# Normalized tokens split over the partition halves, so that the projections run in 64-row tiles of TensorE

## Chip, cores and metric

One core of one Trainium2 chip runs the whole program in one launch. The metric is the device time of that launch in microseconds; the time before is the median of three runs.

## What is computed

A transformer block in fp32 on `x` (2 batches of 1024 tokens, 256 features) with a context of 154 tokens of 192 features. There are 16 heads of 64, so an attention is 1024 wide.

```python
h = layernorm(x, ln1_g, ln1_b)
x = attention(h, h, sa_wq, sa_wk, sa_wv, sa_wo, sa_bo) + x
h = layernorm(x, ln2_g, ln2_b)
x = attention(h, ctx, ca_wq, ca_wk, ca_wv, ca_wo, ca_bo) + x
h = layernorm(x, ln3_g, ln3_b)
p = h @ ff_w1 + ff_b1                      # 2 x 1024 wide
x = (p[..., :1024] * gelu(p[..., 1024:])) @ ff_w2 + ff_b2 + x
# attention: q, k, v by heads; softmax(q k^T / 8) v; then @ wo + bo
```

## The kernel before

**Units.** A unit is one batch and one pair of heads: 16 units, 8 a batch. Self attention takes them in order, and each unit has 8 slots `p` (two halves `h` of 4), so there are 128 slots. In a slot `self_first` (L534) writes two score blocks, each 128 query rows (4 groups of 32) by two heads by 512 keys: 8 matmuls in tiles of 64 rows and 32 columns of TensorE's array (L382), with the head choosing the row half and the bank. The two halves of the keys of one query group lie in different groups of 32 rows, so that maxima and sums are exchanged between partitions by four small DMAs on SP (`exchange`, L403) and joined a slot later (`join`, L407: GpSimd, and an exponential `ee` on ScalarE). VectorE takes the maxima (L542), ScalarE the exponentials (L393), GpSimd scales the weights (L493), VectorE transposes them in blocks of 32 (L507), and two slots behind, `self_values` (L511) multiplies them with the values in 64x64 tiles (`weigh`, L429).

**What fills TensorE between the scores.** In slots 2, 3, 6 and 7 of a unit `self_values` runs for the half before. In slots 0, 1, 4 and 5 (all of the first four slots of all) `run_work` (L452) takes pieces from the list `work`: the projections of the *next* unit, in the order q, q, k, k, v, v (`self_pieces`, L329), each with one PSUM bank of 512 columns (`mm_tile`, two of them in turn). Then, as far as the slot's budget of banks goes, it takes pieces of the output projection from `outs` (L355), and one step of `side`: parts of the next layer norm (`norm_beside`, L267). What a piece leaves in PSUM is copied by ScalarE at the start of the next slot (`stores`, `flush`).

**Projections.** `project_half` (L293) makes queries or keys of 512 tokens: two matmuls of 512 columns over 128 features each, weights stationary, in 128x128 tiles. `project_self_values` (L310) makes 4 token tiles of values: 2 matmuls of 128 columns each, tokens stationary. The values are then copied by two DMAs on SP to the other partition half (L324, L325). An fp32 matmul shows as two records with two weight loads in the profile.

**Layer norm.** `norm_pieces` (L180): statistics by tile of 128 tokens on VectorE, deviation on GpSimd, normalization on ScalarE (L218), four 128x128 transposes for two tiles on TensorE (`turn`, L223), then two stores of 128x256 with gain and shift per partition (L236, L240). The normalized, transposed tokens `hT` have 128 features on the partitions, two chunks of them, and 1024 tokens.

**Weights.** The slices of a unit (256 features by 128 columns, 128 KB for each of q, k, v) come by `load_pair` (L123) into a pool of two buffers, two units ahead, at the unit's first slot (`self_beside`, L554).

**Cross attention.** A unit has three slots with context scores in 64x128 tiles (`cross_first`, L647), 64x64 products with the values (`cross_values`, L721), and the pieces of the next unit: q, q, keys, and values every second unit (`cross_pieces`, L592; `cross_beside`, L756). The feed-forward part follows; its normalized tokens keep their layout.

## Time and profile before

| | us |
|---|---|
| median of three runs (1159.74 to 1162.74) | 1160.25 |
| the profiled execution, its own time | 1161.83 |
| its span | 1160.1 |
| first scores start | 18.4 |
| self attention, units 4 to 14 | 198.7 to 684.7 |
| last unit of self attention | 684.7 to 725.7 |
| cross-attention loop | 725.7 to 961.1 |
| feed-forward | 961.1 to 1160.1 |

TensorE's granted clock was full throughout. A row of a timeline has the start, the length, the engine (PE is a matmul, PEld a weight load), the line, the operation, what it writes and reads, the array tile (64*32 is 64 rows by 32 columns), the shape and the count; in brackets stand idle time before it and what ended it. Matmuls are pipelined and the length of a group contains a modelled tail, so the difference of two starts is what a group takes. A row of a stage table has the stretch, its length, and for each engine its busy time and number of instructions, then granted clock, DMA share and GB/s.

### The profile page before, as it was taken

What the parts mean: (1) busy time and instruction counts of PE and PEld (TensorE: products, weight loads), DVE (VectorE), ACT (ScalarE), POOL (GpSimd) and SP (SyncE); (2) the same over time, 40 slices, a digit from 0 to 9 for tenths busy, and PEclk for the clock granted to TensorE, in tenths of its full rate; (3) what the DMA queues carried; (4) which work ended last, traced back from release to release, by engine and by line L of the source; (5) the groups of instructions that cost most, each with busy time, mean ns of one, the idle gap of its engine ahead of it and who ended that gap; (6) DMA issues with size and microseconds to landing.
All of it is one profiled execution on the core that took longest, in us unless ns stands there. A gap on an engine that the chain in (4) does not pass through costs nothing.

```text
span 1160.1 us, 31720 instructions
## 1 busy us (share of the span) xinstructions
PE 1134.3 (98%) x11931; PEld 675.6 (58%) x11931; DVE 833.0 (72%) x1178; ACT 643.4 (55%) x2055; POOL 665.9 (57%) x1556
## 2 busy tenths in 40 slices
PE   8989999999999999999999999999999999999998
PEld 6334444545545545545445444565666667888887
DVE  4888999898889888888999889557656664232222
ACT  4656677666656665665666766547755572041111
POOL 1767777887877777777777777546654453020000
PEclk9999999999999999999999999999999999999999
DMA  2311011101101111011011010157544433000000
GB/s 76 92 52 34 12 25 35 21 17 31 24 21 22 25 25 21 17 34 21 17 34 21 18 29 5 33 138 195 126 107 103 104 84 71 10 10 10 19 10 18
DMA packets 87250, 51.21 MB, mean 44 GB/s; under 512 B 30830, under 2 KB 77882, under 8 KB 87098
## 3 DMA queue, kind: packets, MB, share of 16 engines
q1 hardware_dynamic: 83738, 46.44, 17.4%
q10 hardware_dynamic: 3360, 2.76, 0.8%
q8 instruction: 94, 1.54, 0.6%
q14 instruction: 58, 0.48, 0.1%
HBM read 19.52 MB, written 2.10 MB: 19 GB/s over the span
## 4 chain that ended last, share of the span: by engine, by line
PE 80%; ACT 7%; DVE 4%; POOL 3%; DMA 2%; issue 2%; SPq 1%; DVEq 0%; ACTq 0%; POOLq 0%
PE po L429 17%; PE s L382 15%; PE pa L824 10%; ACT p L393 5%; PE py_ca L360 5%; PE pf L847 5%; PE py_sa L360 5%; PE pq_ca L299 4%; PE poc L737 4%; PE pk_sa L299 4%; PE pq_sa L299 3%; PE pv_sa L315 3%; PE sc L658 3%; DVE st L542 2%; DMA st<-st 2%
## 5 line engine op out<-in xcount | busy, mean ns | idle before, releaser
L393 ACT ACTIVATE p<-s,st 128x512 f32<-128x512 f32 x512 | 345.2, 686 | 220.7 <-DVE st L542 214.1
L493 POOL TENSOR_SCALAR p<-p,rd,ee 128x512 f32<-128x512 f32 x512 | 385.6, 767 | 44.3 <-DVE rd L489 43.7
L542 DVE TENSOR_REDUCE st<-s 128x2 f32<-128x1024 f32 x256 | 301.3, 1218 | 45.8 <-PE s L382 38.5
L507 DVE STREAM_TRANSPOSE pT<-p 128x1024 f32<-128x1024 f32 x256 | 302.4, 1219 | 1.5 <-POOL p L493 1.5
L382 PE MATMUL s<-k_sa,q_sa 64*32 64x512 f32 x4096 | 253.9, 596 | 14.2 <-ACT p L393 13.1
L429 PE MATMUL po<-pT,v_sa 64*64 64x256 f32 x4096 | 235.8, 379 | 0.0
L429 PEld LDWEIGHTS po<-pT,v_sa 64*64 64x64 f32 x4096 | 150.4, 133 | 109.2 <-issue 38.6
L685 POOL TENSOR_SCALAR p<-p,rden 128x154 f32<-128x154 f32 x256 | 96.8, 399 | 108.8 <-DVE rden L682 108.3
L382 PEld LDWEIGHTS s<-k_sa,q_sa 64*32 64x32 f32 x4096 | 59.9, 105 | 145.1 <-ACT p L393 53.8
L674 ACT ACTIVATE p<-sc,neg 128x154 f32<-128x154 f32 x256 | 96.0, 395 | 83.6 <-DVE rden L682 79.4
L824 PE MATMUL pa<-hT_ln,wf 128*128 128x256 f32 x512 | 121.0, 379 | 0.0
L833 DVE SCALAR_TENSOR_TENSOR u<-pa,cols,gate 128x256 f32<-128x256 f32 x64 | 31.0, 484 | 124.2 <-ACT gate L830 124.2
L830 ACT ACTIVATE gate<-pa,cols 128x256 f32<-128x256 f32 x64 | 30.3, 474 | 151.4 <-PE pa L824 151.4
L824 PEld LDWEIGHTS pa<-hT_ln,wf 128*128 128x128 f32 x512 | 96.8, 190 | 13.7 <-DVE u L833 0.4
L393 ACT ACTIVATION_READ_ACCUMULATOR p<-s,st 128x1 f32 x512 | 103.7, 203 | 0.0
L663 DVE TENSOR_REDUCE neg<-sc 128x6 f32<-128x924 f32 (+1 forms) x48 | 48.5, 1011 | 48.6 <-PE sc L658 48.6
L417 POOL TENSOR_TENSOR zz<-ee,st 128x8 f32<-128x8 f32 x128 | 25.8, 202 | 80.3 <-ACT ee L415 80.3
L315 PEld LDWEIGHTS pv_sa<-sa_wv,hT_ln 128*128 128x128 f32 x512 | 59.1, 192 | 15.8 <-issue 14.1
L847 PE MATMUL pf<-wf,u 128*128 128x256 f32 x256 | 65.0, 379 | 0.2 <-DVE u L833 0.2
L315 PE MATMUL pv_sa<-sa_wv,hT_ln 128*128 128x128 f32 x512 | 62.2, 278 | 0.0
L299 PE MATMUL pq_ca<-hT_ln,ca_wq 128*128 128x512 f32 x128 | 60.0, 608 | 1.6 <-ACT v_ca L632 0.8
L299 PE MATMUL pk_sa<-hT_ln,sa_wk 128*128 128x512 f32 (+1 forms) x132 | 60.5, 596 | 0.6 <-ACT q_sa L308 0.6
(74 smaller groups left out, 1234.6 us busy)
## 6 DMA issues: line engine op xcount, KB each, us to landing
wf<-pT_ca SPq DMA_DIRECT2D x128, 128.0 KB, 2.4
st<-st SPq DMA_DIRECT2D x512, 1.0 KB, 1.7
v_sa<-v_sa SPq DMA_DIRECT2D x64, 128.0 KB, 2.5
wf<-in_L_xattn_ff_w_dram SPq DMA_DIRECT2D x12, 256.0 KB, 3.9
sa_wq<-in_L_xattn_sa_wq_dram SPq DMA_DIRECT2D x16, 128.0 KB, 3.5
sa_wk<-in_L_xattn_sa_wk_dram SPq DMA_DIRECT2D x16, 128.0 KB, 2.3
sa_wv<-in_L_xattn_sa_wv_dram SPq DMA_DIRECT2D x16, 128.0 KB, 2.9
ca_wq<-in_L_xattn_ca_wq_dram SPq DMA_DIRECT2D x16, 128.0 KB, 2.6
```

The costliest lines, as they stand in the source:

```text
L299: nc.tensor.matmul(pq[:, own], lhsT=wt[:, c, :], rhs=h[:, c, n * HB + own.start:n * HB + own.stop], start=(c == 0), stop=(c == NC - 1),)
L315: nc.tensor.matmul(pv[:, i * P:(i + 1) * P], lhsT=h[:, c, (n * GT + i) * P:(n * GT + i + 1) * P], rhs=wt[:, c, :], start=(c == 0), stop=(c ...
L360: nc.tensor.matmul(py[:, :D], lhsT=o[:, i, t * P:(t + 1) * P], rhs=wo[kind][:, half * HP + i, :], start=(i == 0), stop=(i == HP - 1),)
L382: nc.tensor.matmul(sc[a4 * KB:(a4 + 1) * KB, j, :], lhsT=q[r, c:c + KB], rhs=k[r, h * HB:(h + 1) * HB], start=True, stop=True, tile_positi ...
L393: nc.scalar.activation(pr[:, j, :], sc[:, j, :], AF.Exp, bias=st[:, 0, 0, i, j:j + 1], accum_out=st[:, 0, 1, i, j:j + 1],)
L429: nc.tensor.matmul(po[a2][j * DH:(j + 1) * DH, :QH // 2], lhsT=v[r, t, e, j * DH:(j + 1) * DH], rhs=pT[r, j * NK + n, :], start=(t == 0 an ...
L493: nc.gpsimd.tensor_scalar(pr[:, j, :], pr[:, j, :], rd[:, c:c + 1], ee[:, 0, c:c + 1], op0=ALU.mult, op1=ALU.mult,)
L507: nc.vector.transpose(halves[h][:, :, c:c + KB], groups.pop(0).rearrange("p j (n k) -> p (j n) k", k=KB))
L542: nc.vector.tensor_reduce(st[:, 0, 0, i, :], sc[i], AX.X, ALU.max, negate=True)
L685: nc.gpsimd.tensor_scalar(pr_[:, j, i, :T], pr_[:, j, i, :T], rden[:, j, i:i + 1], 1.0, op0=ALU.mult, op1=ALU.mult,)
L824: nc.tensor.matmul(pa[:, half, :TF * P], lhsT=w1[:, c, half * DF + f * P:half * DF + (f + 1) * P], rhs=h[:, c, t0 * P:(t0 + TF) * P], star ...
L847: nc.tensor.matmul(sums[blk][i][:, :D], lhsT=sums[blk, "u"][:, f, i * P:(i + 1) * P], rhs=w2[:, f, :], start=(f == 0), stop=(f == NF - 1),)
```

## The change

The tokens of a batch are split in two halves of 512, and `hT` of the self and context norms becomes four chunks of 64 features: partitions 0 to 63 hold them for the first half of the tokens, partitions 64 to 127 for the second. The transposes stay four for two tiles, since tile i and tile i + 4 are turned together (`tile_order`), and the stores become four of 128x128. Gains and shifts of these two norms are loaded twice, once for each partition half, and so are the slices of the weights, by two DMAs each; their pool goes from two buffers to one.

Queries and keys are projected by `project_both`: for each chunk of 64 features, four groups of 32 output columns and two token halves, a matmul of 512 columns in a 64x32 tile; the two token halves write two banks. In the first unit it uses 64x128 tiles and 256 tokens of each half at a time. Context queries use it in 64x128 tiles, save those of the first context unit, which are made beside self attention, in 64x32. Values are made in 64x128 tiles: tokens of a half stationary, two banks. A piece now has a cost in banks (`costing`), 2 for these pieces, and `run_work` counts it, so that a slot takes one of them. For units 1 to 4 the values stay in two pieces of half the size, with four copy DMAs each; later units have one piece and two larger copies.

The weight loads leave the unit's first slot: `load_ahead` issues q in slot 2, k in slot 3, v in slot 7 of a unit, two units ahead. Context keys and values are loaded one unit ahead, context queries two units ahead in the second of the three slots. The start loads `cols` by four DMAs. In the last self-attention unit two output pieces join `outs` that were listed in the second cross slot before.

```diff
-    wpool = ctx.enter_context(tc.tile_pool(name="w", bufs=2))
+    wpool = ctx.enter_context(tc.tile_pool(name="w", bufs=1))
...
+        t = wpool.tile([P, NH, n], F32, tag=name[3:], name=f"{name}_{c0}")
+        for r0 in range(0, P, HR):
+            nc.sync.dma_start(out=t[r0:r0 + HR], in_=own.rearrange("(c p) f -> p c f", p=HR))
+        return t
...
         def store():
-                for c in range(NC):
-                    own = st["hT"][:, c, t * P:(t + 2) * P]
+                k = NC * 2 * P // nh
+                for c in range(nh):
+                    own = st["hT"][:, c, t // 2 * k:(t // 2 + 1) * k]
...
+    def project_both(dst, pq, wt, h, m, t0=0, n=S // 2, mul=None):
+        for c in range(NH):
+            for f in range(0, P, m):
+                for r in range(2):
+                    own = slice(r * HR, (r + 1) * HR)
+                    nc.tensor.matmul(
+                        pq[r][f:f + m, t0:t0 + n], lhsT=wt[own, c, f:f + m],
+                        rhs=h[own, c, t0:t0 + n], start=(c == 0), stop=(c == NH - 1),
+                        tile_position=(r * HR, f),
+                    )
...
+    def project_self_values(v, pv, wt, h, i0, n):
+        for i in range(i0, i0 + n):
+            for c in range(NH):
+                for r in range(2):
+                    own = slice(r * HR, (r + 1) * HR)
+                    nc.tensor.matmul(
+                        pv[r][:, i * P:(i + 1) * P], lhsT=h[own, c, i * P:(i + 1) * P],
+                        rhs=wt[own, c, :], start=(c == 0), stop=(c == NH - 1),
+                        tile_position=(r * HR, 0),
+                    )
...
+            for own in [slice(0, NT)] if n == GT else tiles:
+                nc.sync.dma_start(out=v[:QG, own, 1, :], in_=v[QG:, own, 0, :])
+                nc.sync.dma_start(out=v[QG:, own, 1, :], in_=v[:QG, own, 0, :])
...
-        for _ in range(min(n, len(work))):
+        while n > 0 and work:
+            n -= work[0].banks
             run(work.pop(0))
-            n -= 1
...
+    def load_ahead(p):
+        ui, n = divmod(p, 2 * SH)
+        for what in "qkv":
+            at = {"q": 2, "k": 3, "v": 2 * SH - 1}[what] + 3 * (ui == 0 and what != "v")
+            if n != at:
+                continue
+            if ui + 2 < NU:
+                load_weights("sa", units[ui + 2][1], what)
+            elif ui + 2 == NU or what == "q":
+                load_weights("ca", units[ui + 2 - NU][1], what)
...
-                full = (hg % 2 == 0 or outs) and p < SA - 2 * SH
-                run_work(2 if full else 1, 1, sum_tile)
+                run_work(2 if p < SA - SH else 1, 1, sum_tile)
...
         if ui + 1 < NU:
+            for what in "kv":
+                load_weights("ca", units[ui + 1][1], what)
             pieces = cross_pieces(*units[ui + 1])
-            work.extend(pieces[:3])
-            held.extend(pieces[3:])
+            work.extend(pieces[:2])
+            held.extend(pieces[2:])
```

## Prediction

> **What bounds the kernel now.** I read the engine shares first, then the busy time by stage, then the order of TensorE's work in time. The engine shares:

> ```profile
> PE 1134.3 (98%) x11931; PEld 675.6 (58%) x11931; DVE 833.0 (72%) x1178; ACT 643.4 (55%) x2055; POOL 665.9 (57%) x1556
> ```

> 98% is an average. The stages (columns: stretch, its length, then busy time of PE, PEld, DVE, ACT, POOL) say where TensorE has room: units 0; 1 to 3; 4 to 14 of self attention; the cross-attention loop.

> ```profile
> 18.40:63.70 45.30, 42.98 (x510) 20.43 (x510) 33.36 (x34) 28.78 (x82) 24.03 (x54) 1.00 0.35 90
> 63.70:198.70 135.00, 127.04 (x1704) 60.07 (x1697) 121.08 (x142) 90.33 (x265) 101.06 (x230) 1.00 0.11 23
> 198.70:684.70 486.00, 485.82 (x6330) 251.78 (x6326) 432.91 (x481) 309.03 (x916) 364.66 (x815) 1.00 0.12 24
> ...
> 725.70:961.10 235.40, 230.26 (x1824) 146.74 (x1821) 146.80 (x326) 142.00 (x619) 124.02 (x346) 1.00 0.47 112
> ```

> From 198.7 on TensorE never rests; DVE has 53 us to spare. In units 1 to 3 PE is idle for 8 us and DVE for 14, so the two take turns. What one TensorE slot is made of, from its timeline (start, length, group):

> ```profile
> 268.59 1.95 PE L382 MATMUL s<-k_sa,q_sa 64*32 64x512 f32 x32
> 270.46 3.72 PE L360 MATMUL py_sa<-sa_wo,o_sa 128*128 128x256 f32 x16
> 274.11 1.95 PE L382 MATMUL s<-k_sa,q_sa 64*32 64x512 f32 x32
> ...
> 285.10 1.95 PE L382 MATMUL s<-k_sa,q_sa 64*32 64x512 f32 x32
> 286.98 3.70 PE L299 MATMUL pq_sa<-hT_ln,sa_wq 128*128 128x512 f32 x8
> 290.61 1.95 PE L382 MATMUL s<-k_sa,q_sa 64*32 64x512 f32 x32
> 292.48 3.70 PE L299 MATMUL pk_sa<-hT_ln,sa_wk 128*128 128x512 f32 x8
> ```

> Read differences of starts; the lengths hold a modelled tail. And where two pieces of one tile form follow each other (no change of form):

> ```profile
> 962.85 3.62 PE L360 MATMUL py_ca<-ca_wo,o_ca 128*128 128x256 f32 x16
> 966.30 1.89 PE L824 MATMUL pa<-hT_ln,wf 128*128 128x256 f32 x8
> ```

> The same 16 records of 256 columns take 3.45 us there (0.842 ns a column) and 3.65 between scores. A change of form in and out costs this piece 0.20. Two score calls are 4 passes of 512 columns, 1.72 us at that rate, and take 1.87: 0.15 more. A query piece is 3.45 at that rate and takes 3.63: 0.18 more. So the two changes of form in a query or key slot cost 0.15 + 0.18 = **0.33 us**.

> [...]

> **The change, part by part.**

> *Queries and keys in 64x32 tiles.* Per unit, 2 x 8 records of 512 columns become 2 x 64, eight at a time: 64/8 x 512 = 4096 columns, 3.45 us as before. Loads grow from 8 to 64 a piece, 32 columns each. The row of the score loads shows that they overlap (4096 of 105 ns in 59.9 us busy):

> ```profile
> L382 PEld LDWEIGHTS s<-k_sa,q_sa 64*32 64x32 f32 x4096 | 59.9, 105 | 145.1 <-ACT p L393 53.8 <-issue 52.9 <-ACT ee L415 29.8
> ```

> Issue: 64 matmuls and 64 loads in 3.45 us is the pace that a po piece already keeps (64 and 64 in 3.62[...]). What goes is both changes: 0.33. Queries and keys issued in units 4 to 14 are 22 pieces, plus unit 15's first context query: 23 x 0.33 = **-7.6 us**. Bounds: 0 (another cause for the 0.33) and 23 x 0.38, if the rate is a little better.
> Who is late next: DVE runs back to back from 81.92 to 86.94, 5.02 us a slot; the query slot falls from 5.50 to 5.17, still above.

> *Context queries in 64x128 tiles, the form of the context scores (sc).* 16 records of 512, two at a time: 3.45 again. They stand between two sc pieces:

> ```profile
> 847.06 1.06 PE L658 MATMUL sc<-k_ca,q_ca 64*128 64x154 f32 x12
> 848.05 3.70 PE L299 MATMUL pq_ca<-hT_ln,ca_wq 128*128 128x512 f32 x8
> 851.68 1.06 PE L658 MATMUL sc<-k_ca,q_ca 64*128 64x154 f32 x12
> ```

> 15 pieces x 0.33 = -5.0. Against it: a piece now needs both banks free before it starts. In the rows of waits pq_ca already waited 0.84 for ACT's v_ca copies and 0.73 for hT, each between the halves of a piece. Now the 1.8 us of first half can't run ahead: about 1 us more, twice. Taken: **-3.0**; bounds -5.7 and 0.

> *Values in 64x128 tiles.* 32 records with 32 loads become 64 and 64, two at a time. Matmuls: 64 x 128 columns x 0.842 / 2 = 3.45. Loads: 3.65 us busy for 32 gives 0.114 each; 64 in pairs need 3.65. Do they pair? sc takes 0.99 with 12 records and 0.72 (856.57 to 857.29) with 8, so 0.067 for one, half of 154 x 0.842 = 0.130 and below 0.114: matmuls and loads of the two row tiles run side by side. Values keep a change of form at both ends. Taken: **0** (3.77 now); bounds -0.2 and +3.6 a unit.

> *Transposed tokens.* Transposes stay 4 a turn; stores go from 2 of 128x256 to 4 of 128x128. ACT: 0.578 less 128 columns at 0.84 ns (0.590 for 512 against 0.375 for 256 in its copies) is 0.47, so a turn costs 1.88 for 1.16: +0.72. In units 12 to 15 and the cross loop ACT's idle time covers it (it waits 2.6 us a slot for DVE's maxima at 304.12); eight turns, **+1.0** for what leaks; bounds 0 and 4.

> *Start.* First turn: four DVE stores at 0.41 (0.54 less 128 x 1.04) for two, +0.56. Last turn: 2 x 0.41 + 2 x 0.47 against 1.10, +0.66. The last key piece waits for it with 512 columns for both halves, 1.72 us instead of 0.86. Together **+2.0**; bounds 0.5 and 3. Two more `cols` issues on ACT end before its table load at 4.02; the table load waits for x.

> *Queues, units 0 to 3.* SP issues 6 weight loads of 0.4 to 0.6 us a unit instead of 3, and 8 value copies of 0.65 instead of 4 up to unit 4 (2 afterwards). The loads leave the unit's first slot, where three together put the exchange late (ACT idle 2.57 us before ee at 64.72). But with one buffer a load waits for the last reader, and behind it on SP stand the exchanges, for which dd, ee and the reciprocal wait. One piece a slot puts 7 pieces in unit 0's 6 slots, so up to unit 4 one lags: the key load is listed a slot before its reader. Floor by the rows: units 1 and 2 with statistics in four slots (DVE 5.54) and four po slots of 5.49, 44.1 each; unit 3 with two half-filled slots at 5.02, 42.3: 130.5 against 135.0. Against these -4.5: four turns at +0.72 where DVE waits for ACT, and 1 us of late exchange in three units. Taken: **0**; bounds -4.5 and +6.
> DMA traffic grows by 16 x 4 loads of 128 KB, 8 MB on 51, where DMA's share is 0.12: hidden behind six slots of lead. Context key and value loads come one unit ahead; SP reaches them 4 us before the unit's first sc, and 12 us before the key piece.

> **Sum.** -7.6 - 3.0 + 0 + 1.0 + 2.0 + 0 = -7.6 us. The profiled execution took 1161.83 for a span of 1160.1; the median shown is 1160.25, 0.1% from either. From the median: **1152.6 us**.

> **Rivals.**
> 1. *Both gains and the early stage relaxes:* [...] units 1 to 3 reach their floor: -8.7 - 4.0 + 3.0 - 4.5 = -14, **1146**. For it: PE's 8 idle us there. Against: DVE is busy 121 of 135.
> 2. *The next wait takes the slot.* Exchange loop: maxima to last exponential 4.04 (302.86 to 306.90), to dd 4.65, dd to reciprocal 1.73: 10.4 for two slots, 5.2 a slot; and a key piece needs both banks while the query copies end 0.2 us before it starts. If slots stay at 5.4, -2.3 and -1.5 remain: +3.0 - 3.8, **1159.5**. For it: these margins. Against: 0.7 of the loop is a bias add, in 16 slots only.
> 3. *It doesn't do what it says:* the 0.33 comes from each piece's start and banks, not its form. Then only the costs are left: **1163**. Against: 3.45 and 3.65 for equal pieces.
> 4. *Slower:* 128-column loads of two row tiles don't overlap in a long piece with accumulation: 64 x 0.114 = 7.3 us, +3.5 in 11 units and some 5 us in the early ones, +44: **1196**. It decides once a load's spacing exceeds 0.059 us. For it: values have as many load columns as matmul columns, with no slack. Against: sc's 0.067 for a record.

> **Numbers.** Forecast 0.50, rival 1 0.17, rival 2 0.14, rival 3 0.10, rival 4 0.09. Within 0.3% (3.5 us) this kernel can't be told from unchanged. Forecast and rival 1 are faster save a tail of 0.04; rival 2 is mostly the same; rival 3 splits. Faster 0.66, same 0.19, slower 0.15. The range 1143 to 1164 takes in rivals 2 and 3 and most of 1; it leaves out rival 4 and a low tail.

> **What would show it.** Right: query slots at about 5.17 (scores to scores), two context units (831.41 to 860.67) 29.26 falling to 28.6, values at 3.8, first scores near 20.4. Wrong: value pieces near 7, query slots at 5.5, new PE waits on ACT copies ahead of pq or pk, ACT idle before ee in units 1 to 4.

## The result, and the profile after

The changed kernel takes **1175.44 us** (median of 4 runs, 1174.99 to 1176.44) against 1159.99 for the kernel before (4 runs, 1159.71 to 1162.74). The ratio is 1.0129, with a 95% interval of 1.0111 to 1.0147: 15 us slower, where 7.6 us faster was forecast, and outside the range. The profiled execution has a span of 1174.6 us and took 1176.44. So 14.5 us of span, against 1160.1, have to be found.

The engine shares, from the page:

```profile
PE 1135.7 (97%) x14343; PEld 684.0 (58%) x14343; DVE 834.8 (71%) x1184; ACT 653.0 (56%) x2095; POOL 666.4 (57%) x1556
```

TensorE's busy time grew by 1.4 us and the span by 14.5: most of the loss is waiting, and part of the busy time turns out to be slower work. Next the same stages as in the prediction (stretch, length, busy time of PE, PEld, DVE, ACT, POOL, then the granted clock): unit 0; units 1 to 3; units 4 to 14; the cross-attention loop.

```profile
20.35:64.45 44.10, 39.94 (x633) 19.79 (x633) 32.41 (x34) 27.92 (x84) 24.02 (x54) 1.00 0.27 68
64.45:204.50 140.05, 129.18 (x2132) 61.03 (x2128) 119.92 (x140) 92.34 (x276) 99.97 (x226) 0.98 0.17 41
204.50:690.70 486.20, 482.78 (x7956) 251.45 (x7952) 434.61 (x482) 314.58 (x933) 366.28 (x818) 1.00 0.15 34
732.90:975.60 242.70, 233.72 (x1945) 152.06 (x1942) 147.22 (x326) 144.11 (x627) 124.07 (x347) 0.98 0.48 117
```

In units 1 to 3 PE's idle time went from 8.0 to 10.9 us, in the cross loop from 5.1 to 9.0, and in these two stages the clock column fell from 1.00 to 0.98. The stages by the starts of the score calls, in us (a stage ends where the next one starts):

```
stage          before    after   change   of it forecast
first scores    18.42    20.35    +1.9    +2.0
units 0 to 4   222.52   229.00    +6.5    -0.7
units 5 to 12  353.26   348.40    -4.9    -5.3
units 13, 14    90.47    92.97    +2.5    -1.3 and most of +1.0
unit 15         41.05    42.18    +1.1    -0.3
cross 0 to 3    65.39    66.67    +1.3    -1.3
cross 4 to 6    40.30    49.08    +8.8    -1.0 and +2.0
cross 7 to 15  129.71   126.90    -2.8    -2.6
feed-forward   198.94   199.09    +0.2     0
```

The steady stages do what was forecast. A query and a key slot, from TensorE's timeline:

```profile
294.88 3.64 PE L327 MATMUL pq_sa<-hT_ln,sa_wq 64*32 64x512 f32 x64
298.31 1.92 PE L442 MATMUL s<-k_sa,q_sa 64*32 64x512 f32 x32
300.03 3.64 PE L327 MATMUL pk_sa<-hT_ln,sa_wk 64*32 64x512 f32 x64
303.46 1.92 PE L442 MATMUL s<-k_sa,q_sa 64*32 64x512 f32 x32
```

Scores to scores is 5.15 here (5.17 in the query slot), for 5.51 before; the value slot keeps its 5.65. The loss is elsewhere, and the rows of PE's waits name its places (us in total, times, longest):

```profile
PE s L442 <- ACT p L453: 18.2, 34, 3.5
PE pq_ca L327 <- ACT hT_ln L258: 3.0, 2, 2.7
PE pk_ca L675 <- DMA ca_wk<-in_L_xattn_ca_wk_dram: 2.5, 1, 2.5
...
PE pq_ca L327 <- ACT v_ca L701: 1.9, 1, 1.9
```

Before, the rows of these places were the following, and there was none for the DMA:

```profile
PE s L382 <- ACT p L393: 13.1, 31, 1.3
...
PE pq_ca L299 <- ACT v_ca L632: 0.8, 1, 0.8
PE pq_ca L299 <- ACT hT_ln L240: 0.7, 1, 0.7
```

Together these rows grew by 11 us; what else was lost shows only when one such wait is followed in time. In cross unit 4 (row tiles 0 and 1 are the two halves of 64 rows of TensorE's array; the piece writes one bank for each):

```profile
800.46 1.02 PE L327 MATMUL pq_ca<-hT_ln,ca_wq 64*128 64x512 f32 x2
803.37 4.96 PE L327 MATMUL pq_ca<-hT_ln,ca_wq 64*128 64x512 f32 x13 [1.89 <-ACT v_ca L701]
807.75 0.68 PE L728 MATMUL sc<-k_ca,q_ca 64*128 64x154 f32 x4
808.18 0.59 PE L327 MATMUL pq_ca<-hT_ln,ca_wq 64*128 64x512 f32 x1
808.61 0.94 PE L728 MATMUL sc<-k_ca,q_ca 64*128 64x154 f32 x8
```

The first matmul of row tile 0 (two records) runs, the first of row tile 1 waits 1.89 us for its bank. Then the next scores start 4.4 us later (803.37 to 807.75), where run 5 below takes 2.7 for the same records. The reason is the clock. Three windows of 3.41 us around this wait, and two around the one of 2.73 us in cross unit 5 (PE's busy time is the first figure after the length; the clock stands before the last two):

```profile
800.02:803.43 3.41, 1.52 (x14) 0.69 (x10) 3.31 (x10) 2.19 (x6) 3.16 (x9) 1.00 0.99 227
803.43:806.84 3.41, 3.41 (x8) 1.46 (x10) 0.00 (x0) 2.08 (x12) 1.13 (x4) 0.50 0.39 91
806.84:810.26 3.42, 3.42 (x36) 2.31 (x36) 0.67 (x1) 1.20 (x2) 0.00 (x0) 1.00 0.04 10
817.08:820.50 3.42, 0.69 (x3) 0.30 (x4) 1.79 (x4) 3.42 (x14) 3.17 (x9) 1.00 1.03 249
820.50:823.91 3.41, 3.41 (x10) 1.39 (x8) 0.00 (x0) 1.68 (x10) 0.35 (x2) 0.50 0.20 55
```

PE was idle for 1.89 us of one window, and in all of the next it got half its clock. This happens at 73.0 (two windows), 742.0, 803.4 and 820.5 us: 17 us at half clock, up to 8.5 us of work lost. The profile of the kernel before has none of it between its start and its end.

How the early wait arises, unit 1 (SP's queue, POOL, ACT and PE):

```profile
57.90 1.37 SPq L130 DMA_DIRECT2D sa_wq<-in_L_xattn_sa_wq_dram  x2
59.38 0.62 SPq L365 DMA_DIRECT2D v_sa<-v_sa  x1
...
62.61 3.39 SPq L463 DMA_DIRECT2D st<-st  x4
...
66.11 1.35 SPq L130 DMA_DIRECT2D sa_wk<-in_L_xattn_sa_wk_dram  x2
...
67.31 0.20 POOL L471 TENSOR_TENSOR dd<-st 128x4 f32<-128x4 f32 x1 [3.48 <-DMA st<-st]
...
67.61 2.47 SPq L463 DMA_DIRECT2D st<-st  x4
...
68.04 0.21 ACT L475 ACTIVATE ee<-dd 128x8 f32<-128x8 f32 x1 [3.15 <-POOL dd L473]
68.05 0.37 ACTq L120 DMA_DIRECT2D sa_wo<-in_L_xattn_sa_wo_dram  x1
...
70.19 1.34 SPq L130 DMA_DIRECT2D sa_wv<-in_L_xattn_sa_wv_dram  x2
...
71.90 1.09 PE L442 MATMUL s<-k_sa,q_sa 64*32 64x512 f32 x16 [3.51 <-ACT p L453]
...
74.41 0.20 POOL L471 TENSOR_TENSOR dd<-st 128x4 f32<-128x4 f32 x1 [2.28 <-DMA st<-st]
```

An exchange issued from 62.61 on is there for dd at 67.31, ACT stands 3.15 us at ee, its next exponentials come late, and the scores wait 3.51 us for the buffer that these free. SP came to this exchange late because it issued two query loads and four value copies first (57.90 to 62.45); ACT's last exponential before it had ended at 59.31. Once issued, the exchange was quick: its last DMA started at 65.41 and was there 1.9 us later, and the median of all exchanges is 1.8. The next exchange is late for another reason: its last DMA started at 69.49, 1.4 us after the 1024 KB load of the output weights (68.05), and dd got it 4.9 us later.

### The profile page after: what moved, and what is told of

Same layout as the page of the kernel before. It is cut to its first block, busy times and chain, and to the rows that moved or that the text cites. A ratio compares the mean times of both kernels' runs of the same rounds, so it can differ in the third digit from the quotient of the medians.

```text
span 1174.6 us, 36750 instructions
## 1 busy us (share of the span) xinstructions
PE 1135.7 (97%) x14343; PEld 684.0 (58%) x14343; DVE 834.8 (71%) x1184; ACT 653.0 (56%) x2095; POOL 666.4 (57%) x1556
## 4 chain that ended last, share of the span: by engine, by line
PE 72%; ACT 9%; DMA 5%; POOL 4%; DVE 3%; SPq 3%; issue 3%; ACTq 0%; DVEq 0%; POOLq 0%
PE po L489 14%; PE s L442 12%; PE pa L894 9%; ACT p L453 6%; PE py_ca L420 5%; PE pq_ca L327 5%; PE pf L917 5%; PE py_sa L420 4%; DMA st<-st 4%; PE poc L807 4%; PE pv_sa L352 3%; PE sc L728 3%; PE pq_sa L327 3%; SPq L463 2%; PE pk_sa L327 2%
## 5 line engine op out<-in xcount | busy, mean ns | idle before, releaser
L453 ACT ACTIVATE p<-s,st 128x512 f32<-128x512 f32 x512 | 344.9, 687 | 201.8 <-DVE st L602 198.7
L442 PE MATMUL s<-k_sa,q_sa 64*32 64x512 f32 x4096 | 257.1, 597 | 19.3 <-ACT p L453 18.2
L442 PEld LDWEIGHTS s<-k_sa,q_sa 64*32 64x32 f32 x4096 | 63.8, 106 | 145.8 <-ACT p L453 68.7
L352 PEld LDWEIGHTS pv_sa<-sa_wv,hT_ln 64*128 64x128 f32 x1024 | 59.6, 188 | 19.9 <-issue 8.4
L327 PE MATMUL pq_ca<-hT_ln,ca_wq 64*128 64x512 f32 (+1 forms) x304 | 64.9, 616 | 5.1 <-ACT hT_ln L258 3.0
L477 POOL TENSOR_TENSOR zz<-ee,st 128x8 f32<-128x8 f32 x128 | 25.9, 202 | 73.6 <-ACT ee L475 73.6
L352 PE MATMUL pv_sa<-sa_wv,hT_ln 64*128 64x128 f32 x1024 | 64.0, 276 | 1.8 <-ACT k_sa L341 1.2
L549 DVE RECIPROCAL rd<-den 128x4 f32<-128x4 f32 x128 | 22.6, 177 | 57.2 <-POOL den L479 51.7
```

The costliest lines, as they stand in the source:

```text
L327: nc.tensor.matmul(pq[r][f:f + m, t0:t0 + n], lhsT=wt[own, c, f:f + m], rhs=h[own, c, t0:t0 + n], start=(c == 0), stop=(c == NH - 1), tile ...
L352: nc.tensor.matmul(pv[r][:, i * P:(i + 1) * P], lhsT=h[own, c, i * P:(i + 1) * P], rhs=wt[own, c, :], start=(c == 0), stop=(c == NH - 1), ...
L442: nc.tensor.matmul(sc[a4 * KB:(a4 + 1) * KB, j, :], lhsT=q[r, c:c + KB], rhs=k[r, h * HB:(h + 1) * HB], start=True, stop=True, tile_positi ...
L453: nc.scalar.activation(pr[:, j, :], sc[:, j, :], AF.Exp, bias=st[:, 0, 0, i, j:j + 1], accum_out=st[:, 0, 1, i, j:j + 1],)
```

## The experiments

Times are medians; all runs were made beside runs of the kernel before, whose medians were 1160.0 to 1161.1. "After" is the changed kernel, 1175.44, and every edit is to it unless it says so. DMA timing and the phase of the clock windows differ from one execution to the next (the wait for `ca_wk`, where nothing was edited, is 2.5 us in the profile after, 2.3 in run 7 and 2.2 in run 6; a window begins at 803.43 us in the profile after and at 818.88 in that of run 3, 4.53 windows of 3.413 us apart), so a single profile's stages scatter where nothing was edited: most by some tenths, units 13 and 14 by up to 0.7, and a stage by 1.7 more where a half-clock window comes or goes. Units 0 to 4 scatter most: runs 2, 3 and 5, which edit nothing there, have 228.0, 231.0 and 232.3 for 229.0. Where the interval of a run overlaps that of the changed kernel (runs 1, 3, 5, 6 and 7), its total proves nothing alone, and the argument goes by the places in the traces.

**1. The forms of queries and keys undone.**

```diff
-                t[what], t["bank"], wsl["sa", pr, what], t["h"], P if first else KB, i * n, n,
+                t[what], t["bank"], wsl["sa", pr, what], t["h"], P, i * n, n,
-        nxt = ... else cross_pieces(*units[0], KB)
+        nxt = ... else cross_pieces(*units[0])
```

> Queries and keys of every self-attention unit after the first, and the first context query, in 64x128 tiles again, which is not the form of the scores beside them; nothing else differs from the changed kernel. Theory (the 0.33 us of a query or key slot is the price of two changes of tile form): 23 pieces at 0.33, so about 7.6 us slower than the changed kernel, 1183, with query slots of units 5 to 11 back at 5.50 us (scores to scores). Rival (the 0.33 belongs to the number of loads or the start of a piece): the slots stay at 5.17 and the time at 1175.

Measured: 1178.08 (1.0151 of before, 1.0131 to 1.0171). The slots answer clearly:

```profile
301.47 1.95 PE L442 MATMUL s<-k_sa,q_sa 64*32 64x512 f32 x32
303.35 3.70 PE L327 MATMUL pk_sa<-hT_ln,sa_wk 64*128 64x512 f32 x16
306.99 1.95 PE L442 MATMUL s<-k_sa,q_sa 64*32 64x512 f32 x32
```

5.52 from scores to scores, with the same two row tiles and two banks; each unit from 6 to 11 takes 44.17 for 43.44 (43.58 in one). So 0.36 us is the price of the two changes of form in a slot. The total rose by 2.6 and not by 7.6: units 0 and 1 were 2.4 us shorter, units 13 and 14 1.8, and cross unit 4 lost its half clock (1.7). That slower slots left those stages more room is a likely reading, not shown; unit 4 drew a half-clock window of its own. The saving is real where TensorE sets the pace; that it is smaller where TensorE waits anyway is argued.

**2. Copies and stores of the cross loop on VectorE.**

```diff
-                    nc.scalar.copy(v[own, n, :], pv[own, :VC])
-                nc.scalar.copy(v[:KB, NM, :], pv[:KB, VC:])
+                    nc.vector.tensor_copy(v[own, n, :], pv[own, :VC])
+                nc.vector.tensor_copy(v[:KB, NM, :], pv[:KB, VC:])
-                    if first and (c < nh // 2 or t % 4 == 0):
+                    if (kind, b) == ("ca", B - 1) or first and (c < nh // 2 or t % 4 == 0):
```

> In the cross-attention loop the three copies of the context values out of their bank, and the four stores of a transposed turn, go from ScalarE to VectorE. Theory (the 8.8 us of cross units 4 to 6 come from a query piece that needs both banks while one of them waits behind the normalizing on ScalarE, and from the lower TensorE clock that follows each such wait): the three units fall back by 7 to 9 us, the stretches at half clock near 803 and 820 us are gone, total 1166 to 1168. Rival (only the waits cost; the clock is incidental, or VectorE becomes as late as ScalarE): 4 us or less, and the half-clock stretches stay.

Measured: 1195.26 (1.0297, 1.0271 to 1.0323). The theory missed. The rival had the cause (VectorE becomes as late as ScalarE, and the half-clock stretches stay) but not the size. Cross units 4 to 6 went to 52.4, and six even units (2, 6, 8, 10, 12, 14) lost 2.7 to 4.4 us each. Cross unit 6:

```profile
834.37 1.12 DVE L733 TENSOR_REDUCE neg<-sc 128x6 f32<-128x924 f32 x1 [0.67 <-PE sc L728]
...
835.40 0.86 DVE L700 COPY v_ca<-pv_ca 64x256 f32<-64x256 f32 x2
...
836.30 0.41 DVE L701 COPY v_ca<-pv_ca 32x256 f32<-32x256 f32 x1
...
836.81 5.40 PE L327 MATMUL pq_ca<-hT_ln,ca_wq 64*128 64x512 f32 x14 [2.49 <-issue]
```

The value copies now stand on DVE behind the maxima of the next scores, and the query piece waits for them ("issue", since the row names no releaser). It isn't the engine's load that counts (DVE has 95 us free in this loop) but what stands ahead of a bank's copy in its order.

**3. The second context keys loaded earlier.**

```diff
+            if p == SA - SH + 2:
+                load_weights("ca", units[1][1], "k")
-            for what in "kv":
+            for what in ("v" if ui == 0 else "kv"):
```

> The key weights of the second context unit are asked for two slots before the end of self attention rather than at the first slot of the cross loop. Theory (the load stood on SP behind exchanges and value copies, the key piece waited 2.45 us for it and the clock was halved for 3.4 us after it): cross unit 0 falls by 1.5 to 4 us, no half clock at 742 us; total 1171.5 to 1174. Rival (the slot is set by other waits of that stage, such as the last exchanges): the wait moves to another row and the time stays at 1175.

Measured: 1173.69 (1.0110, 1.0089 to 1.0131). Cross unit 0 fell by 2.28 and the next rose by 0.66; no half clock at 742. The wait for the load is gone; the key piece waits 1.06 us for ACT's query copies in its place, as the rival said. How much the load's place costs by itself stays open: runs 8 and 11 leave the load where it was, wait 1.7 us for it, have no half clock there and take 12.0 us in cross unit 0, no more than the 12.1 here. Most of the 2.28 is then the clock. Of more use is what happened by chance in cross unit 5, whose code is untouched: the same wait of 2.73 us, but no half clock.

```profile
820.49 3.27 PE L327 MATMUL pq_ca<-hT_ln,ca_wq 64*128 64x512 f32 x13 [2.73 <-ACT hT_ln L258]
```

```profile
815.47:818.88 3.41, 2.29 (x18) 1.29 (x16) 2.93 (x8) 3.41 (x14) 3.18 (x9) 1.00 0.90 240
818.88:822.30 3.42, 1.81 (x8) 0.88 (x10) 0.52 (x1) 3.42 (x16) 2.35 (x7) 1.00 0.86 192
822.30:825.71 3.41, 3.41 (x36) 2.33 (x36) 0.70 (x1) 1.56 (x4) 0.00 (x0) 1.00 0.02 6
```

A window boundary cut the wait into 1.13 and 1.61 us (3.41 less the busy figures), and after neither did the clock fall (1.00 in both windows that follow). The 13 records took 3.27 instead of 4.96 and the unit 16.58 instead of 18.26: **1.68 us is what the halved clock costs**, on top of the wait.

**4. Values of units 1 to 4 in one piece.**

```diff
-        parts = 2 if ui < HP else 1
+        parts = 1
```

> The values of units 1 to 4 in one piece with two copies between the halves, as later units have them, rather than in two pieces with four copies. Theory (units 0 and 1 lose 6 us because SP has seven pieces' copies and loads ahead of the exchanges, and the piece that lags lists the key load late): units 0 to 4 fall by 4 to 6 us, no wait of 3.5 us at 68 us and no half clock after it; total 1169 to 1171. Rival (the loss comes from the four stores of a transposed turn on ScalarE and from the statistics, whatever SP does): 1 us or less.

Measured: 1167.32 (1.0059, 1.0037 to 1.0081), 8.1 us less than after: more than expected, but not where it was expected. Units 0 to 4 fell by only 0.9, cross unit 0 by 4.3. Counting the records of the output pieces explains it: in the changed kernel a half piece of values lags into unit 4, so no output piece fits there, each later unit does the pieces of the one before, and two of them (16 records, 3.65 us) remain for cross unit 0. With one piece they are back in unit 4. So units 0 to 4 do 3.65 us more work in 0.9 us less time: a gain of some 4.6, with the scatter of that stage on it. A half-clock window still follows a wait of 2.2 us at 73.6, ahead of a key piece that waits for the query copies.

**5. Waits filled.**

```diff
+            banks = two_banks(f"pq_ca{b}_{pr}")
+            for _ in range({5: 2, 6: 3}.get(b * NPAIR + pr, 0)):
+                nc.tensor.matmul(
+                    banks[0], lhsT=wsl["ca", pr, "q"][:HR, 0, :], rhs=hT["ca", b][:HR, 0, :],
+                    start=True, stop=True, tile_position=(0, 0))
...
+            for _ in range(4 if (b, pr) == (0, 1) else 0):
+                nc.tensor.matmul(
+                    pk[:, :B * TP], lhsT=ident[:CC, :], rhs=ctxT[:, 0, :], start=True, stop=True)
```

> Matmuls that nothing reads are put ahead of three pieces that wait: two of 64x512 ahead of the query piece of context unit 5, three ahead of that of unit 6, four of 96x320 ahead of the key piece of unit 1. They write the bank that is free already and are overwritten. The waits are filled, not removed. Theory (a wait of about 1.9 us or more in one window of 3.41 us halves the clock in the next window, which costs 1.7 us on top of the wait): no half clock near 742, 803 and 820 us, about 1.7 us less at each place, 3 to 5 us in all, total 1170.5 to 1172.5. Rival (the clock falls for another reason, or the fill delays what it stands ahead of): 1175 or more.

Measured: 1173.77 (1.0111, 1.0090 to 1.0132). At the places themselves: cross unit 4 less 1.70, unit 5 less 1.70, unit 0 less 1.15, no half clock at any of the three. In cross unit 4 (the line of the added matmuls is L671):

```profile
802.69 1.88 PE L671 MATMUL pq_ca<-hT_ln,ca_wq 64*128 64x512 f32 x4
804.40 1.02 PE L327 MATMUL pq_ca<-hT_ln,ca_wq 64*128 64x512 f32 x2
805.60 3.27 PE L327 MATMUL pq_ca<-hT_ln,ca_wq 64*128 64x512 f32 x13 [0.18 <-ACT v_ca L709]
808.28 0.68 PE L736 MATMUL sc<-k_ca,q_ca 64*128 64x154 f32 x4
```

The bank comes no earlier (2.91 us after the start of the first row in both runs), and yet the next scores come after 2.7 us and not 4.4. The total shows only 1.7 of the 4.6, since in this profile units 0 and 4 drew half-clock windows that the other one didn't have (+1.8 and +1.9).

**6. Two stores for a turn.**

```diff
-                for c in range(nh):
-                    own = st["hT"][:, c, t // 2 * k:(t // 2 + 1) * k]
+                    for c in range(0, nh, 2):
+                        nc.scalar.activation(
+                            st["hT"][:, c:c + 2, t // 2 * k:(t // 2 + 1) * k], ph[:, c:c + 2, :],
...
```

> A transposed turn of the later units is stored in two pieces of 128x256 instead of four of 128x128; each piece takes one gain and one shift for two groups of features, so the numbers differ from the reference's. Theory (the four stores on ScalarE are what units 13 to 15 lose, 3.6 us, and part of what units 1 and 2 lose): units 13 to 15 fall by 2 to 3 us, cross unit 5 by 1 to 2, total 1169 to 1171. Rival (the loss there is the wait of the normalizing for VectorE, whatever the stores cost): units 13 to 15 keep 47.2, 45.8 and 42.2, and the time stays within 1.5 us of 1175.

Measured: 1171.10 (1.0097, 1.0065 to 1.0128). Units 13 and 14 fell by 1.4, unit 15 not at all, cross units 4 to 6 by 2.2 (the wait for hT 1.8 for 2.7). The two extra stores cost 3.6 us in these two places (3.0 if units 13 and 14 are taken from runs 2, 3, 5 and 7, which don't edit them), nearer the prediction's upper bound of 4 than its 1.0; but they aren't all of units 13 to 15. Unit 15's +1.1 is no loss: the two output pieces that it carries now stood in the cross loop before.

**7. The output weights loaded in unit 2.**

```diff
-        later.append(lambda: load_out("sa", nc.scalar))
+            if p == 20:
+                load_out("sa", nc.scalar)
```

> The load of the output weights, 512 KB, is asked for in unit 2 rather than in the slot at 68 us, where the changed kernel has it beside the key and value weights of unit 2; before, it stood at 56.7 us. Theory (an exchange asked for at 67.6 us lands at 74 us [...], and the query copies and the key piece wait behind it): the wait of 2.3 to 3.5 us in unit 1 shrinks by 2 us or more, no half clock near 73 us, total 1170 to 1172. Rival (the exchange is late because SP reaches it late, behind the value copies and weight loads): no more than 0.5 us less.

Measured: 1175.00 (1.0127, 1.0108 to 1.0145): nothing gained. The load has 1024 KB by the profile's rows of DMA issues (the expectation's 512 was wrong). Unit 1 fell by 3.7, unit 2 rose by 5.0, with slots of 9.6 and 8.2. In its new place the load is issued at 139.79, and an exchange issued at 142.1 lands after 5.4 us; before, one issued at 57.8, 1.0 us behind the same load, took 5.7. So the load held up an exchange behind it in both places (the median is 1.7 to 1.8), and moved whole it took that loss along. It can't have caused the wait of 3.51 us shown above: that exchange had landed (67.31) before the load was issued (68.05). It bears on the slot after it, which took 9.26 us and here 6.87.

**8. Offsets one step earlier.** VectorE makes the offset of a norm a step ahead of ScalarE's normalizing; in the cross loop a turn's stores are listed ahead of the next normalizing.

```diff
-        for fns, first in ((turn, 3), (stats, 0), (deviation, 1), (normalize, 2)):
+        for fns, first in ((turn, 3 + more), (stats, 0), (deviation, 1),
+                           *((o, 2) for o in offset), (normalize, 2 + more)):
...
+                    if turns and kind == "ca" and b == B - 1:
+                        done.pop()()
```

> In the norms beside self and cross attention the offset that VectorE makes for the normalizing is made one step earlier than the normalizing on ScalarE, and in the cross loop the stores of a turn are listed ahead of the next normalizing. No work is added. Theory (the query pieces of cross units 4 to 6 wait for a bank because ScalarE stands 1.8 us at the normalizing for VectorE with the copies behind it): the waits of 1.9 and 2.7 us fall below 1, no half clock there, cross units 4 to 6 fall by 5 to 8 us; units 13 to 15 fall too, by 1 to 2; total 1166 to 1170. Rival (the bank is late because of the four stores themselves, or the exponentials): under 2 us.

Measured: 1169.98 (1.0084, 1.0067 to 1.0100). Cross units 4 and 5 fell by 3.4 and 3.6; the waits of 1.89 and 2.73 became none and 0.57:

```profile
813.74 1.02 PE L340 MATMUL pq_ca<-hT_ln,ca_wq 64*128 64x512 f32 x2
815.33 3.27 PE L340 MATMUL pq_ca<-hT_ln,ca_wq 64*128 64x512 f32 x13 [0.57 <-ACT hT_ln L265]
```

So the banks were late because of the order of the steps on VectorE and ScalarE; which of the two reorderings did it, one run of both doesn't tell. Cross unit 6 keeps its 15.1 for 13.6 before: a wait of 0.61 for the turn's stores and a trailing record of row tile 1 at the end of the piece. Units 13 and 14 gained 0.8, hardly more than their scatter.

**9. Repairs 3, 4, 7 and 8 together.**

> Four repairs at once: values of units 1 to 4 in one piece, the early load of the second context keys, the later load of the output weights, the earlier offsets. Theory: the losses are separate places on one path, so the gains add: 6 to 8, 1.5 to 3.5, 3 and 6 from 1175.4, total 1156 to 1160, at or below the kernel before. Rival (a repaired place uncovers the next wait): 1162 to 1167.

Measured: 1164.01 (1.0034, 1.0020 to 1.0048), the rival's figure. The single gains (1.7, 8.1, 0.4, 5.5) add to 15.7 and give 11.4. What was left: units 0 to 4 at 227.5 for 222.5 before.

**10. The same with the output weights in eight loads of 128 KB**, one every second slot of units 1 and 2, and the early offsets in the cross loop alone.

```diff
+            if 9 <= p < 9 + 2 * NPAIR and p % 2:
+                i = (p - 9) // 2
+                nc.scalar.dma_start(out=wo["sa"][:, i, :], in_=w["sa_wo"][i * P:(i + 1) * P, :])
```

> Values of units 1 to 4 in one piece; early load of the second context keys; earlier offsets in the cross loop alone; and the output weights, 1024 KB, in eight loads of 128 KB, one every second slot of units 1 and 2. Theory (one load of 1024 KB holds up an exchange wherever it stands, eight small ones do not): units 0 to 3 fall by 3 to 4 us against the run with four repairs, total 1159 to 1161. Rival (the early units lose by every weight load and by the two-bank pieces, not by the one big load): 1163 to 1165.

Measured: 1160.79 (12 runs; 1.0003, 0.9993 to 1.0012): as fast as the kernel before. Units 0 to 4 take 225.3, units 0 to 3 fell by 2.2 and not by 3 to 4. That eight small loads cost less than the big one is the likely reading; it isn't shown apart, since this run also drops the early offsets beside self attention.

**11. No weight loads in units 0 and 1.**

```diff
-            if ui + 2 < NU:
+            if ui < 2:
+                wsl["sa", ui + 2, what] = wsl["sa", 1, what]
+            elif ui + 2 < NU:
```

> The changed kernel without the weight loads that it asks for in units 0 and 1: units 2 and 3 use the weights of unit 1, so the output is not the reference's. The output weights stay where they are. Theory (SP's time and the bulk traffic of the weight loads between the exchanges make the loss of units 0 and 1): these two fall by 4 us or more, total 1169 to 1171.5. Rival (the value copies, the 1024 KB load and the two-bank pieces make it): under 2 us, 1173.5 to 1175.5.

Measured: 1168.76 (1.0067, 1.0050 to 1.0084), 6.7 less than after. Units 0 and 1 fell by 4.8, and no wait for exponentials is over 1.5. The theory holds: 128 KB loads between exchanges, with the 1024 KB load beside them, make the early waits. SP's own time and the traffic can't be told apart by this run; in the profile after, shown above, it was SP's time for the first late exchange and traffic for the second. A rival is the pool with one buffer, where a load waits for the last reader and the exchanges stand behind it on SP. No run went back to two buffers, but SP's queue in the profile after speaks against it here: up to 72 us no weight load stood more than 1.0 us at such a wait, and none beside these exchanges more than 0.42 (one at 97.74 us stood 2.77).

**12. Empty slots filled, on top of run 10.** Two matmuls of 128x512 that nothing reads, in slot 5 of units 2 and 3, where there is no piece to do, and in the third slot of the cross loop.

> The run with the spread output weights, and two matmuls of 128x512 that nothing reads in each of three places where its trace shows TensorE with no piece to do and a half-clock window after it: slot 5 of units 2 and 3, and the third slot of the cross loop. Theory (the idle time there is another engine's and stays, the halved clock after it does not): about 1.5 us less at each place, 3 to 5 in all, total 1156 to 1158, below both kernels. Rival (the filling delays the scores or the next piece as much as the clock gives back): 1160 to 1162.

Measured: 1160.86 (13 runs; 1.0000, 0.9991 to 1.0009): no gain in the total. In units 2 and 3 it did what it should. Without and with it:

```profile
140.29 1.95 PE L455 MATMUL s<-k_sa,q_sa 64*32 64x512 f32 x32
144.30 1.09 PE L455 MATMUL s<-k_sa,q_sa 64*32 64x512 f32 x16 [2.06 <-ACT p L466]
```

```profile
139.79 1.95 PE L455 MATMUL s<-k_sa,q_sa 64*32 64x512 f32 x32
141.67 1.98 PE L1000 MATMUL fill<-hT_ln,ident 128*128 128x512 f32 x4
143.81 1.09 PE L455 MATMUL s<-k_sa,q_sa 64*32 64x512 f32 x16 [0.15 <-ACT p L466]
```

The slot after it falls from 7.61 to 5.98, in unit 3 from 7.22 to 5.98. In cross units 0 to 3 the time rose by 1.4: that the filler stands in the wrong place there, a slot behind the idle time that lowers the clock, is a likely reading, not shown. This and unit 1 (+1.1) took the gain back.

**13 and 14. The eight small loads in units 2 and 3; and beside it the values in two pieces again.** Neither fills anything in the cross loop.

> As the filled run, but the eight small loads of the output weights stand in units 2 and 3, after the last token loads, and nothing is filled in the cross loop. Theory (bulk loads between the exchanges are what is left of the early loss): the wait of 3.4 us in unit 1 goes, units 0 to 3 fall by 1.5 to 3 us, the total is 1157 to 1159, below both kernels. Rival (the early units are set by ScalarE and VectorE with statistics and two-bank pieces, and the wait only changes its place): 1160 to 1162.

> As the run with the later output weights, but the values of units 1 to 4 in two pieces with four copies, as in the changed kernel. Theory (the lagging piece and its copies cost some 5 us by themselves): 1162 to 1165. Rival (one piece only helped by moving the other loads): within 1 us of the run beside it.

Measured: 1162.49 (21 runs; 1.0016, 1.0009 to 1.0023) and 1165.52 (5 runs; 1.0040, 1.0028 to 1.0052). The first missed, and lies above its rival's range too: 2.7 us of idle time in one window of unit 1 stay without the output weights near it, so they aren't due to these. What exactly they belong to is open; no run took away the token loads of units 0 and 1 or SP's value copies alone. The second says that the lagging half piece costs 3.0 us by itself when the other places are repaired (8.1 when they aren't).

No version beat both kernels. The best equals the kernel before.

## Why the prediction was wrong, step by step

- **Queries and keys, -7.6: right.** 5.50 became 5.17 and 5.15, units 5 to 12 gained 4.9 of a forecast 5.3, and run 1 gives it back.
- **Context queries, changes of form -5.0: right; the two-bank wait, +2.0: the step that failed.** Two units went from 29.26 to 28.47 (28.6 forecast). But "about 1 us more, twice" was +10.0 in cross units 4 to 6: 8.8 measured, and 1.2 of saving gone under it. I took the old waits of 0.84 and 0.73 and added the half piece that could no longer run ahead. That gives the first wait (1.84, measured 1.89) but not the second (1.73, measured 2.73): run 6 brings the second to 1.8, so the other 0.9 came from the four stores of a turn. A third place (1.4 in unit 6) was missing, and so was the halved clock that follows such a wait (1.7, twice). Runs 3, 5, 6 and 8 show the parts. No run gave the two row tiles of a query piece one bank, so what the two banks are worth isn't shown.
- **Values, 0: right.** The slot is 5.65 as before. Rival 4 is out: loads of two row tiles overlap in a long piece too (64 loads of 128 columns and 64 matmuls in 3.77 us, by starts).
- **Transposed tokens, +1.0: mis-sized.** 3.0 to 3.6 us by run 6, near the upper bound. More than half lies in the cross loop, on the bank that the query piece waits for: idle time of ACT on average was no cover, because the store stands between a piece and its bank.
- **Start, +2.0: right in its sum**, +1.9; its parts weren't measured apart, save that a store of 128 columns on VectorE takes 0.40 us, for the 0.41 reckoned from the 0.54 of 256 columns.
- **Queues and units 0 to 3, 0: wrong.** +6.5 in units 0 to 4, which moreover did two output pieces less: some 10 us. The ingredients were named (the lagging piece, loads ahead of exchanges), but set against a floor that needs all of them to be on time. Runs 14 and 4 put 3.0 and 8.1 us on the lagging piece, and run 11 puts 5 on the weight loads near the exchanges; these overlap, and how the 10 us divide stays open.
- **Context keys "12 us before the key piece": wrong for cross unit 0.** SP reached that load at 738.34, behind exchanges and value copies, 5.4 us after the first context scores; the piece waited 2.45 and the clock fell. The figure came from the steady units; the first one has another queue ahead of it. Run 3 takes 2.3 us less there, but so do runs 8 and 11 with the load in its place and no half clock: most of it is the clock.
- **Not in the sum at all:** the clock. It was full in the profile before, and the prediction gave a new wait no price beyond its length. Three of its places measured 1.15, 1.7 and 1.7 us; the one at 73 us, of two windows, was not measured by itself.

Rival 2 (a new wait takes the gain) came nearest in kind, but in its place and its size it was another: it looked at the exchanges of the steady slots, which fell to 5.17 and 5.15 all the same. None of the rivals put a loss of this size in the places where it lay.

## What to carry to other kernels

A change that saves a little in every slot is judged by the slots that aren't steady: first units, changes of stage, slots with a norm beside them. When a piece comes to need two buffers at once, list for each buffer what stands ahead of its last reader on that engine, for every unit and not for the typical one. And a TensorE wait of about 2 us cost up to 1.7 us more than its length here, so a new wait of that size is worth a fill or a reordering, while two of 1 us may cost only themselves (after 0.8 to 1.38 us of idle time in a window the clock stayed full in 91 of 91 cases, see below).

## What the runs showed of the hardware

```
PE idle in a window   windows   next one at half clock
0.8 to 1.38 us           91       0
1.39 to 1.84 us          35       8
1.89 us and more         39      39
```

- So the same wait of 2.73 us cost 1.7 us more or nothing more, by where a window boundary cut it (run 3). The executions of one kernel differ in their clock too: run 1's four had granted clocks of 0.992, 0.996, 0.997 and 0.999 and took 1180.3, 1179.5, 1176.1 and 1176.7 us.
- **Behind a half-clock window less was enough.** With 0.59 to 1.54 us of idle time in it, it was followed by another one in 11 of 11 cases; with 0 to 0.50 us in 1 of 48. So unit 1 has two in a row (72.98 to 79.80): 0.70 us of idle time fell into the first.
- Where an interleaved piece waited behind its first two records (1.89 us above, 0.18 in run 5), one record of row tile 1 trailed into the scores that follow (808.18 above, 808.71 in run 5), and they went on 0.43 us after its start in both.
- One load of 1024 KB delayed 1 KB exchanges that another queue issued: it stood on ACT's queue, the exchanges on SP's, and one issued 1.0 to 2.3 us behind it took 5.7 us (before) and 5.4 us (run 7) to land, where the median is 1.7 to 1.8.
